# A stack of four layers with a state-space scan: C's rows through DRAM, softplus as one ScalarE function, and one program without a loop

## The chip, the cores and the metric

The kernel runs on one core of one Trainium2 chip. The metric is the device time of one execution in microseconds. "Profiled execution" means one execution that the hardware profiler recorded; its "span" runs from the first to the last instruction.

## The reference

The input is 32 images of 128 channels and 56 x 56 pixels, in float32. Each image passes four layers. Before each layer the image is normalized over groups of channels.

1. A dynamic convolution: the channel means choose a mixture of four 128 x 128 matrices, and the result goes through one depthwise 3 x 3 kernel at dilations 1, 3 and 5, with a silu after each.
2. A spline of every pixel's value.
3. A linear attention over an 8 x 8 grid, with a depthwise convolution.
4. A Mamba layer over the 3136 pixels in order. The change lies here. Cut to what matters:

```python
xc = silu(conv1d(xin) + conv_b)                   # 256 inner channels
dbl = xc @ x_proj_w.T                             # 8 columns dt, 16 of B, 16 of C
delta = softplus(dbl[:, :8] @ dt_proj_w.T + dt_proj_b)
dA  = exp(delta[..., None] * A)                   # 256 channels x 16 states
dBu = delta[..., None] * B[:, :, None, :] * xc[..., None]
h_t = dA_t * h_{t-1} + dBu_t                      # along the pixels
y_t = einsum('bdn,bn->bd', h_t, C_t)
out = ((y + xc * D) * silu(z)) @ out_proj_w.T
```

## The kernel before

**Chunks and steps.** An image is cut into 7 chunks (`NCH`) of 448 pixels (`CH`), 224 chunks in all. The scan of a chunk takes 16 steps (`STEPS`): 256 channels in two halves (`db`, 0 or 1), and 16 states in 8 pairs (`p`). In one step the 128 partitions hold 64 channels twice, once for each state of the pair, and two such blocks stand side by side, so that a tile is 128 x 2 x 448. A step does this:

- `b_rows`: TensorE spreads the two rows of B over the 128 partitions, from `dbl` (the high and the low parts of dt, B and C, as float32r) by a selection matrix `sel`, into the one PSUM buffer `pb`.
- `decay`: ScalarE makes the two `da` tiles, exp(delta times A), in three PSUM buffers.
- `state`: VectorE multiplies `du` (delta times x) by `pb` into `h`, and scans `h` twice along the pixels.
- `products`: ScalarE saves the last column, and GpSimd multiplies `h` by the rows of C (`cb`) into `hc`.
- `add`: TensorE sums `hc` over the states into `y`. After the last pair of a half VectorE multiplies by the gate, `sz`.

In the steps of the first half `c_rows` also makes the `cb` tile of a pair: TensorE spreads the rows of C by `sel` as it does B's, and ScalarE copies the result from PSUM into one of nine buffers (`NPAIR + 1`). The second half uses the same eight tiles.

**The inputs of the next chunk.** `ssm_inputs` (line 989) prepares the next chunk during the steps of this one: the convolution and silu give `xc`, a matmul gives `dbl`, and softplus gives `delta`. Softplus is made as max(v, 0) on VectorE plus ln(1 + exp(-|v|)): Abs, Exp and Ln on ScalarE, and a sum on GpSimd, which also multiplies by `xc`. All of this stands on 128 different channels in the partitions. So 16 transfers within SBUF of 64 rows (112 KB each) then bring `delta` and `du` into the doubled form. `layer_norm` for the chunk after is put between, so that its Ln shares one switch of ScalarE's function table with that of softplus.

**Order.** Nothing is issued as it is written. `Plan` records every instruction with a price (`price`, line 163) and a step at which it is wanted, and then writes out one order for each engine: it takes, for each engine, what can start first by its prices. Each engine carries out its queue in that order. While the scan of one image goes on, the plan fills in the spline and attention of the next image (`rest`) and the first layer of the image after that (`layer0`). `PREP` says how the pieces of `ssm_inputs` are spread over the steps. All instructions that were recorded so have one line number in the profile, 325.

**DMA.** All transfers are issued by SP. Convolutions read their rows from DRAM (`padded`) into `stack`, as four transfers each, the last being a single row of ones (`onesd`); the spline reads 16 transfers of 32 rows from `xt`.

**Images.** The first image and the first layer of the second come ahead. Then a loop on the device (line 1263) runs five times over six images each (`UNROLL`), and the last two images follow it:

```python
    with tc.For_i(0, B - 2, unroll) as i:
        images(i, unroll, True)
    images(B - 2, 2, False)
```

The functions that the change touches, and those that call them:

Of the kernel before, what the change touches and what calls it, by code (L numbers as in the profile page):

```python
# [26 lines left out]
PW = W + 2 * HALO  # L27
UNROLL = 6

PREP = 17.5  # L30
REST = 92
# [63 lines left out]
class Plan:  # L95
# [67 lines left out]
    def price(self, w, engine, method, args, kw):  # L163

        n = args[0].free_size()
        if method == "dma_start":
            w.cost += 0.35
            w.bytes += 4 * n * args[0].partition_size()
        elif engine == "tensor":
            n = args[2].free_size() if method == "matmul" else n  # L170
            w.cost += max(0.06, n * (5e-4 if args[2].dtype == F32R else 1.8e-3))
        elif engine == "scalar":
            if method == "activation" and args[2] in (AF.Exp, AF.Tanh, AF.Ln):
                w.table = "ln" if args[2] == AF.Ln else "exp"
            columns = sum(isinstance(kw.get(k), bass.AP) for k in ("bias", "scale"))
            w.cost += 0.06 + 8.34e-4 * n + 0.09 * columns + 0.03 * (args[1].space != bass.MemoryType.PSUM)
        elif engine == "gpsimd":
            if n <= 8:
                w.cost += 0.52 if ALU.pow in args else 0.15
            else:  # L180
                slow = method != "tensor_scalar" or ALU.add not in args
                w.cost += 0.14 + n * (1.2e-3 if not slow else 2.12e-3 if method != "tensor_scalar" else 3.8e-3)
        elif method == "tensor_tensor_scan":
            w.cost += 0.11 + 2.085e-3 * n
        else:
            if method == "tensor_reduce" or method == "bn_stats":
                n = args[1].free_size()
            w.cost += 0.08 + 1.02e-3 * n
# [161 lines left out]
def tile_conv_stack(ctx: ExitStack, tc: tile.TileContext, out: bass.AP, x: bass.AP, w: dict):  # L350
# [44 lines left out]
    xprojT = load("xprojT", [P, DI, P])  # L395
    dtb = load("dtb", [P, DI])
    amat = load("alog", [P, NB, NPAIR])
# [15 lines left out]

    ones4 = const.tile([P, NST], F32, name="ones4")
    nc.vector.tensor_add(ones4[:], ident[:, 0:NST], ident[:, LOW : LOW + NST])
    for r in (C_ROW, C_ROW + LOW):
        nc.vector.tensor_add(ones4[:], ones4[:], ident[:, r : r + NST])
    sel = const.tile([P, NST, Q], F32R, name="sel")
    nc.vector.tensor_copy(sel[:], ones4[:].unsqueeze(2).to_broadcast([P, NST, Q]))

    low = load("low", [P, 2])
    dtT = const.tile([P, DI * P], F32R, name="dtTr")
    dtw = setup(DI * P, name="t")
    nc.sync.dma_start(dtw[:], w["dtT"])
    nc.vector.tensor_copy(dtT[:], dtw[:])
    nc.vector.scalar_tensor_tensor(dtT[:], dtT[:], low[:, 1:2], dtw[:], ALU.mult, ALU.add)

# [96 lines left out]

    cbT = const.tile([P, DI * P], F32R, name="cbT")
    cbw = setup(DI * P, name="g")
    nc.vector.memset(cbw[:], 0.0)
    for r in (0, 32):
        nc.sync.dma_start(cbw[r : r + 1, :], w["convb"])
    nc.vector.tensor_scalar_mul(cbw[:], cbw[:], 0.5)  # L530
    nc.vector.tensor_copy(cbT[:], cbw[:])
    nc.vector.tensor_sub(cbT[32:33, :], cbw[32:33, :], cbT[32:33, :])
    onesr = const.tile([P, 1], F32R, name="onesr")
# [7 lines left out]
    xns = [const.tile([P, CH + DCONV - 1], F32, name=f"xn{k}") for k in range(3)]  # L541
    dbls = [const.tile([P, CH], F32R, name=f"dbl{k}") for k in range(2)]
    xcs = [const.tile([P, DI, CH], F32, name=f"xc{k}") for k in range(2)]
    halves = [[const.tile([P, 2, CH], F32, name=f"{n}{k}") for k in range(3)] for n in ("delta", "du")]

    sz = const.tile([P, DI, CH], F32, name="sz")
    delta = const.tile([P, DI, CH], F32, name="delta")
    du = const.tile([P, DI, CH], F32, name="du")

    padded = [dramp.tile([P, PW * PW], F32, name=f"padded{k}") for k in range(2)]
    onesd = dramp.tile([1, NG * ROWS * PW], F32, name="onesd")
    zero = setup(HALO * PW, name="t")
    nc.vector.memset(zero[:], 0.0)
# [9 lines left out]

    plan.pitch = {pd[:].tensor.name: PW * PW for pd in padded} | {onesd[:].tensor.name: NG * ROWS * PW}
    nc = plan

# [375 lines left out]
    def norm_weights(st, ctr, cb):  # L944
# [5 lines left out]
        nc.vector.tensor_scalar_mul(cb[:], pm, -1.0)  # L950
    def layer_norm(xt, xn, j, norm, before=None, other=None):


        if norm is None:
            nc.scalar.activation(other, other, AF.Ln, bias=one[:, 0:1])
            return
        ctr, cb = norm
# [8 lines left out]
        rstd = tmp.tile([P, CH], F32, tag="v", name="rstd")  # L966
        with plan.together():
            nc.scalar.activation(rstd[:], pv, AF.Ln, bias=lneps[:, 0:1])
            if other is not None:
                nc.scalar.activation(other, other, AF.Ln, bias=one[:, 0:1])  # L970
            nc.scalar.activation(rstd[:], rstd[:], AF.Exp, scale=-0.5)
        nc.gpsimd.tensor_mul(rstd[:], cen[:], rstd[:])
# [16 lines left out]
    def ssm_inputs(xt, k, norm):  # L989
# [3 lines left out]
        for db in range(DI):  # L993
            ch = slice(db * P, (db + 1) * P)
            ps = psum()
            for i in range(DCONV):
                nc.tensor.matmul(ps, winT[:, i, ch], xn[:, i : i + CH], start=(i == 0), stop=False)
            nc.tensor.matmul(ps, cbT[:, ch], onesr[:].to_broadcast([P, CH]), start=False, stop=True)
            silu(xc[:, db, :], ps)
            yield 3.3  # L1000
        ps = psum()
        for db in range(DI):
            nc.tensor.matmul(ps, xprojT[:, db, :], xc[:, db, :], start=(db == 0), stop=(db == DI - 1))
        nc.scalar.copy(dbl[:], ps)
        nc.vector.scalar_tensor_tensor(dbl[:], dbl[:], low[:, 0:1], ps, ALU.mult, ALU.add)
        yield 1.7

        for db in range(DI):
            ps = psum()
            nc.tensor.matmul(ps, dtT[:, db * P : (db + 1) * P], dbl[:], start=True, stop=True)  # L1010
            nc.scalar.activation(du[:, db, :], ps, AF.Abs, bias=dtb[:, db : db + 1])
            nc.vector.tensor_scalar(delta[:, db, :], ps, dtb[:, db : db + 1], 0.0, ALU.add, ALU.max)
            yield 0.8
        nc.scalar.activation(du[:], du[:], AF.Exp, scale=-1.0)
        layer_norm(xt, xns[(k + 1) % 3], j + 1, norm if j + 1 < NCH else None, xn, du[:])
        nc.gpsimd.tensor_add(delta[:], delta[:], du[:])
        nc.gpsimd.tensor_mul(du[:], delta[:], xc[:])
        yield 4.0

        for db in range(DI):  # L1020
            for src, dst in zip((delta, du), halves):
                dst = dst[(DI * k + db) % 3]
                for s in range(2):
                    for r in range(2):
                        nc.sync.dma_start(dst[Q * s : Q * s + Q, r, :], src[Q * r : Q * r + Q, db, :])
        yield 1.0

    class Scan:
# [11 lines left out]

        def both(self, ps, row, p):

            rows = slice(row, row + 2 * LOW)
            pair = sel[rows, 2 * p : 2 * p + 2, :].rearrange("p a b -> p (a b)")
            nc.tensor.matmul(ps, pair, self.dbl[rows, :], start=True, stop=True)

        def c_rows(self, n):

            db, p = divmod(n, NPAIR)
            if db == 0:  # L1050
                ps = psum()
                self.both(ps, C_ROW, p)
                self.cbs[p] = cbp.tile([P, CH], F32, tag="cb", name="cb")
                nc.scalar.copy(self.cbs[p][:], ps)

        def b_rows(self, n):

            p = n % NPAIR
            self.pbs[n] = ps_bc.tile([P, 512], F32, tag="bc", name="pb")[:, :CH]
            self.both(self.pbs[n], B_ROW, p)  # L1060

# [113 lines left out]
    ov = out.rearrange("b c l -> c b l")  # L1175
    unroll = next(u for u in (UNROLL, 2) if (B - 2) % u == 0)

# [84 lines left out]
    plan.issue()  # L1262
    with tc.For_i(0, B - 2, unroll) as i:
        images(i, unroll, True)
    images(B - 2, 2, False)


def _layout(a):
# [21 lines left out]
    def xproj_columns(v):  # L1290
        m = np.zeros((DI * P, P), np.float32)
        for h in (0, LOW):
            for r in DT_ROWS:
                m[:, h + r : h + r + DTR] = v[:, :DTR]
            m[:, h + B_ROW : h + B_ROW + NST] = v[:, DTR : DTR + NST]
            m[:, h + C_ROW : h + C_ROW + NST] = v[:, DTR + NST :]
        return m

    def dt_rows(v):
        m = np.zeros((P, DI * P), np.float32)  # L1300
        for h in (0, LOW):
            for r in DT_ROWS:
                m[h + r : h + r + DTR] = v
        return m

    def low_rows():
        m = np.zeros((P, 2), np.float32)
        for h in (0, 2 * LOW):
            m[h + LOW : h + 2 * LOW, 0] = -1.0
        for h in (0, LOW):  # L1310
# [28 lines left out]
        "low": low_rows(),  # L1339
        "dtb": halves(a["L3_conv_dt_proj_b"]),  # L1340
        "alog": pairs(a["L3_conv_A_log"]),
# [26 lines left out]
```

## Time and profile before

| | |
|---|---|
| Time, median of 3 runs | 17185.76 us (17185.5 to 17192.23) |
| Profiled execution, time | 17194.07 us |
| Its span | 17192.1 us |
| TensorE matmul busy | 14998.2 us, 87% |
| VectorE busy | 14452.2 us, 84% |
| ScalarE busy | 11730.3 us, 68% |
| GpSimd busy | 10788.9 us, 63% |
| DMA, mean over 16 engines | 39.0% of the span, 92 GB/s |
| Mean granted TensorE clock | 0.885 |

In the profile PE is TensorE, PEld its weight loads, DVE VectorE, ACT ScalarE, POOL GpSimd, and SPq the queue of SP, which issues the transfers. An instruction is named by what it writes and reads, `out<-in`. A group's row gives its shape and number, then the busy time in us and the mean ns of one, then the idle time of its engine just before, with what ended that idle time. The row of a window gives, for each engine, busy time and instructions, and at the end the granted clock, the mean share of the 16 DMA engines and GB/s. The part of the span before the loop takes about 495 us, each turn of the loop about 3150 us, and the last two images the rest.

### The profile page before, as it was taken

Reading aid. Unit: us, or ns where it says so; the run is one execution under the profiler, and the core shown is the slowest. Engines: PE = TensorE matmul, PEld = TensorE weight load, DVE = VectorE, ACT = ScalarE, POOL = GpSimd, SP = SyncE. Lnnn points to the kernel's source line nnn. Section 1 sums busy time; section 2 is a strip of 40 time slices with the busy share of each in tenths; the row PEclk is TensorE's granted clock in tenths of the full one; section 3 lists DMA queues with packets and bytes.
Section 4 is the critical chain, followed back from the end, with each engine's and each line's share of the span. In section 5 each row is a group of like instructions: output and inputs, shape, how many; then the busy total and the mean of one; then the engine's idle time right before and its main releaser. Section 6 shows DMA issues by size and latency. Waiting matters only on the chain. (4 is left out here: it accounts for less than half of the span.)

```text
span 17192.1 us, 216067 instructions
## 1 busy us (share of the span) xinstructions
PE 14998.2 (87%) x68192; PEld 4866.0 (28%) x68192; DVE 14452.2 (84%) x17314; ACT 11730.3 (68%) x21127; POOL 10788.9 (63%) x6406
## 2 busy tenths in 40 slices
PE   6888998888988888988889888889888898888888
PEld 1222222222222222222222222222222222222222
DVE  2788888888888888888888888888888888888889
ACT  3666677766677666777666776667776667766675
POOL 1566666666666666666666666666666666666666
PEclk7888898989998888989899888899888999888887
DMA  4443443434433444434344334444343443344421
GB/s 105 105 96 94 101 98 84 98 89 97 106 89 87 96 96 97 100 84 98 91 96 106 93 82 96 95 102 98 85 97 88 98 106 91 85 98 95 94 55 31
DMA packets 986167, 1590.09 MB, mean 92 GB/s; under 512 B 175621, under 2 KB 611208, under 8 KB 984330
## 3 DMA queue, kind: packets, MB, share of 16 engines
q1 hardware_dynamic: 985002, 1576.06, 39.0%
q8 instruction: 548, 8.98, 0.2%
q14 instruction: 617, 5.05, 0.1%
HBM read 785.62 MB, written 173.18 MB: 56 GB/s over the span
## 5 line engine op out<-in xcount | busy, mean ns | idle before, releaser
L325 POOL TENSOR_TENSOR hc<-h,cb 128x896 f32<-128x896 f32 x3584 | 7480.6, 2092 | 5035.7 <-DVE h L325 2490.3
L325 DVE TENSOR_TENSOR_SCAN h<-da,last,h 128x448 f32<-128x448 f32 x6144 | 6811.5, 1138 | 628.5 <-ACT da L325 530.6
L325 ACT ACTIVATE da<-delta,alog 128x448 f32<-128x448 f32 x7168 | 4490.6, 633 | 2043.6 <-DVE h L325 1843.0
L325 DVE TENSOR_TENSOR h<-du,pb 128x896 f32<-128x896 f32 x3584 | 3838.3, 1071 | 422.3 <-PE pb L325 179.9
L325 PE MATMUL y<-hc,sums 128*64 128x448 f32 x14336 | 3937.6, 628 | 283.7 <-POOL hc L325 279.3
L325 PE MATMUL pb<-dbl,sel 64*128 64x448 f32 x3584 | 1841.4, 514 | 626.6 <-DVE h L325 584.6
L325 PE MATMUL mm<-xn,winT 128*128 128x448 f32 x3584 | 1782.4, 605 | 172.0 <-DVE sz L325 129.5
L325 PE MATMUL mm<-stack,dsT 96*32 96x448 f32 (+1 forms) x16128 | 1877.0, 576 | 58.2 <-DMA stack<-onesd 23.5
L325 ACT ACTIVATE hats<-stack,bia,scl 128x448 f32<-128x448 f32 x2688 | 1894.2, 755 | 13.0 <-DVE bia L325 10.0
L325 PE MATMUL mm<-hats,wspl 128*32 128x448 f32 x12544 | 1476.4, 574 | 130.7 <-DVE xt L325 68.5
L325 PEld LDWEIGHTS pb<-dbl,sel 64*128 64x128 f32 x3584 | 714.6, 199 | 2985.3 <-DVE h L325 1877.5
L325 PEld LDWEIGHTS y<-hc,sums 128*64 128x64 f32 x14336 | 800.6, 146 | 2063.1 <-issue 971.8
L325 ACT ACTIVATE t<-mm 128x448 f32<-128x448 f32 x1568 | 816.5, 536 | 791.0 <-PE mm L325 780.4
L325 ACT COPY cb<-mm 128x448 f32<-128x448 f32 x1792 | 927.9, 529 | 568.0 <-PE mm L325 456.2
L325 PE MATMUL mm<-dbl,sel 64*128 64x448 f32 x1792 | 874.1, 517 | 476.1 <-ACT cb L325 139.4
L325 ACT ACTIVATE hats<-hats,one 128x1344 f32<-128x1344 f32 x896 | 1261.2, 1408 | 1.2
L325 ACT COPY last<-h 128x2 f32<-128x2 f32 x3072 | 579.0, 188 | 815.6 <-DVE h L325 790.3
L325 DVE TENSOR_TENSOR_SCAN h<-da,h 128x448 f32<-128x448 f32 x1024 | 1064.3, 1074 | 54.5 <-ACT da L325 46.5
L325 POOL TENSOR_TENSOR xt<-xt,g 128x448 f32<-128x448 f32 x672 | 765.1, 1139 | 341.9 <-DVE g L325 330.4
L325 PEld LDWEIGHTS mm<-xn,winT 128*128 128x128 f32 x3584 | 613.1, 199 | 1026.5 <-issue 662.5
L325 DVE SCALAR_TENSOR_TENSOR g<-t,mm 128x448 f32<-128x448 f32 x672 | 410.5, 611 | 406.1 <-ACT t L325 403.4
L325 PEld LDWEIGHTS mm<-stack,dsT 96*32 96x32 f32 (+1 forms) x16128 | 429.6, 113 | 1127.7 <-issue 875.2
(187 smaller groups left out, 15891.8 us busy)
## 6 DMA issues: line engine op xcount, KB each, us to landing
stack<-padded SPq DMA_DIRECT2D x2688, 264.0 KB
stack<-xt SPq DMA_DIRECT2D x3584, 56.0 KB
delta<-delta SPq DMA_DIRECT2D x1792, 112.0 KB
du<-du SPq DMA_DIRECT2D x1792, 112.0 KB
padded<-yc SPq DMA_DIRECT2D x224, 264.0 KB
padded<-yc SPq DMA_DIRECT2D x256, 231.0 KB
xt<-x_dram SPq DMA_DIRECT2D x224, 224.0 KB
out_dram<-xt SPq DMA_DIRECT2D x224, 224.0 KB
```

Of the source, the lines that this page charges most:

```text
L325: call()
```

## The change

**C's rows.** `dbl` keeps dt and B alone, in 64 partitions. The 16 rows of C are copied by ScalarE into `ct` and written to DRAM (`crow`, two buffers); each `cb` tile is then read from there by one transfer, which repeats each of two rows for 64 partitions.

**Softplus.** The weights of dt are doubled beforehand, so that a matmul gives the doubled form at once: four matmuls per chunk where there were two, and a ScalarE function Softplus straight into the `delta` that the scan reads. Only `xc` is doubled by DMA (`xds`, eight transfers of 64 rows per chunk), and GpSimd makes `du` from both. `layer_norm` moves ahead of this and no longer shares a group with softplus.

**Images.** `images(0, B, False)` records all 32 images as one plan; there is no loop on the device.

**Prices.** The plan's price of a float32r matmul is raised, softplus has a table of its own in it, and `PREP` is 16.0.

```diff
-UNROLL = 6
-PREP = 17.5
+PREP = 16.0
...
-            w.cost += max(0.06, n * (5e-4 if args[2].dtype == F32R else 1.8e-3))
+            w.cost += 0.16 + 5e-4 * n if args[2].dtype == F32R else max(0.06, 1.8e-3 * n)
...
+    crows = [dramp.tile([NST, CH], F32, name=f"crow{k}") for k in range(2)]
...
-        with plan.together():
-            nc.scalar.activation(rstd[:], pv, AF.Ln, bias=lneps[:, 0:1])
-            if other is not None:
-                nc.scalar.activation(other, other, AF.Ln, bias=one[:, 0:1])
-            nc.scalar.activation(rstd[:], rstd[:], AF.Exp, scale=-0.5)
+        nc.scalar.activation(rstd[:], pv, AF.Ln, bias=lneps[:, 0:1])
+        nc.scalar.activation(rstd[:], rstd[:], AF.Exp, scale=-0.5)
...
             silu(xc[:, db, :], ps)
+            with plan.together():
+                for h in range(2):
+                    for r in range(2):
+                        nc.sync.dma_start(xds[db][Q * h : Q * h + Q, r, :], xc[Q * r : Q * r + Q, db, :])
...
-        nc.scalar.copy(dbl[:], ps)
-        nc.vector.scalar_tensor_tensor(dbl[:], dbl[:], low[:, 0:1], ps, ALU.mult, ALU.add)
+        ct = tmp.tile([P, CH], F32, tag="v", name="ct")
+        nc.scalar.copy(ct[C_ROW : C_ROW + NST, :], ps[C_ROW : C_ROW + NST, :])
+        nc.sync.dma_start(crows[k % 2][:], ct[C_ROW : C_ROW + NST, :])
+        nc.scalar.copy(dbl[:], ps[: 2 * LOW, :])
+        nc.vector.scalar_tensor_tensor(dbl[:], dbl[:], low[: 2 * LOW, 0:1], ps[: 2 * LOW, :], ALU.mult, ALU.add)
         yield 1.7
+        if j + 1 < NCH:
+            layer_norm(xt, xns[(k + 1) % 3], j + 1, norm, xn)
+        yield 3.0
         for db in range(DI):
-            ps = psum()
-            nc.tensor.matmul(ps, dtT[:, db * P : (db + 1) * P], dbl[:], start=True, stop=True)
-            nc.scalar.activation(du[:, db, :], ps, AF.Abs, bias=dtb[:, db : db + 1])
-            nc.vector.tensor_scalar(delta[:, db, :], ps, dtb[:, db : db + 1], 0.0, ALU.add, ALU.max)
-            yield 0.8
-        nc.scalar.activation(du[:], du[:], AF.Exp, scale=-1.0)
-        layer_norm(xt, xns[(k + 1) % 3], j + 1, norm if j + 1 < NCH else None, xn, du[:])
-        nc.gpsimd.tensor_add(delta[:], delta[:], du[:])
-        nc.gpsimd.tensor_mul(du[:], delta[:], xc[:])
-        yield 4.0
-
-        for db in range(DI):
-            for src, dst in zip((delta, du), halves):
-                dst = dst[(DI * k + db) % 3]
-                for s in range(2):
-                    for r in range(2):
-                        nc.sync.dma_start(dst[Q * s : Q * s + Q, r, :], src[Q * r : Q * r + Q, db, :])
-        yield 1.0
+            delta, du = (h[(DI * k + db) % 3] for h in halves)
+            for r in range(2):
+                b = 2 * db + r
+                ps = psum()
+                nc.tensor.matmul(ps, dtT[:, b * P : (b + 1) * P], dbl[:], start=True, stop=True)
+                nc.scalar.activation(delta[:, r, :], ps, AF.Softplus, bias=dtb[:, b : b + 1])
+            nc.gpsimd.tensor_mul(du[:], delta[:], xds[db][:])
+            yield 1.5
...
             if db == 0:
-                ps = psum()
-                self.both(ps, C_ROW, p)
                 self.cbs[p] = cbp.tile([P, CH], F32, tag="cb", name="cb")
-                nc.scalar.copy(self.cbs[p][:], ps)
+                rows = crows[self.k % 2][2 * p : 2 * p + 2, :]
+                nc.sync.dma_start(self.cbs[p][:], rows.unsqueeze(1).to_broadcast([2, Q, CH]))
...
-    with tc.For_i(0, B - 2, unroll) as i:
-        images(i, unroll, True)
-    images(B - 2, 2, False)
+    images(0, B, False)
```

## The prediction

> **What bounds the kernel now.** I read the page first: the busy times and the DMA queues.
>
> ```profile
> PE 14998.2 (87%) x68192; PEld 4866.0 (28%) x68192; DVE 14452.2 (84%) x17314; ACT 11730.3 (68%) x21127; POOL 10788.9 (63%) x6406
> ...
> q1 hardware_dynamic: 985002, 1576.06, 39.0%
> ```
>
> Two engines are nearly full: TensorE at 87%, VectorE at 84%. Over 224 chunks the span is 76.75 us per chunk, VectorE works 64.5 us of it, and each of the 16 DMA engines is busy 0.39 x 76.75 = 29.9 us. Next the timeline, for the distance from one `h<-du,pb` to the next: averaged over all chunks, steps 0 to 6 of a chunk take 3.6 to 4.7 us, steps 7 to 13 take 4.7 to 5.1, steps 14 and 15 take 5.7 and 6.7. A step needs 1071 + 2 x 1138 ns = 3.35 us of VectorE before any other work, so the early steps have no slack on VectorE; most of its 12 us of idle time per chunk lies in the late ones. So what leaves VectorE pays, what leaves another engine pays only through a wait of VectorE. The chain of waits covers only the last quarter of the span (it adds up to 23%) and mixes TensorE, VectorE and ScalarE, so I do not build on it.
>
> The groups by form (busy us, mean ns, then idle before them):
>
> ```profile
> L325 DVE TENSOR_TENSOR_SCAN h<-da,last,h 128x448 f32<-128x448 f32 x6144 | 6811.5, 1138 | 628.5 <-ACT da L325 530.6 <-ACT cb L325 0.5 <-ACT last L325 0.5
> L325 ACT COPY cb<-mm 128x448 f32<-128x448 f32 x1792 | 927.9, 529 | 568.0 <-PE mm L325 456.2 <-PE pb L325 105.1 <-POOL hc L325 2.7
> L325 PE MATMUL mm<-dbl,sel 64*128 64x448 f32 x1792 | 874.1, 517 | 476.1 <-ACT cb L325 139.4 <-DVE g L325 92.8 <-ACT cen L325 78.3
> L325 ACT ACT_TABLE_LOAD x512 | 656.9, 1283 | 8.8
> L325 DVE TENSOR_SCALAR delta<-mm,dtb 128x448 f32<-128x448 f32 x448 | 298.5, 677 | 166.7 <-ACT du L325 150.3 <-PE mm L325 11.5
> L325 ACT ACTIVATE du<-mm,dtb 128x448 f32<-128x448 f32 x448 | 276.7, 632 | 322.2 <-PE mm L325 287.0 <-DMA stack<-xt 20.5 <-DVE delta L325 11.1
> L325 PE MATMUL mm<-dbl,dtTr 128*128 128x448 f32 x448 | 210.7, 495 | 20.9 <-ACT cen L325 13.9 <-DVE dbl L325 1.3
> ```
>
> The fifth row disappears with the change, with the 166.7 us that VectorE stood idle before it; rows two, three and six price what ScalarE and TensorE lose and gain. Then VectorE's waits and those of SP's queue (total, times, longest):
>
> ```profile
> DVE h L325 <- ACT da L325: 577.0, 443, 4.4
> ...
> DVE h L325 <- DMA du<-du: 104.2, 43, 4.7
> ```
>
> ```profile
> SPq L325 <- DMA stack<-padded: 287.5, 337, 4.3
> ```
>
> ScalarE's `da` is the largest wait of VectorE; SP already waits for landings of its own earlier transfers.
>
> **The change, part by part.** The sum is made against the profiled execution, 17194.07 us, which is 8 us over the median. About 0.2% is what a measurement of this kernel can tell from no change.
>
> VectorE: 448 `delta` instructions go, 298.5 us, all on the path. Of the 166.7 us idle before them I take half, since the wait for ScalarE may reappear at the next instruction: -298 - 83 = -381 us (ends -298 and -465).
>
> ScalarE: the copies of `cb` (927.9 us), Abs (276.7), Exp (213.0) and Ln (231.6) go, 1649 us. Added: 896 softplus at the 632 ns of `du<-mm,dtb`, the same shape with a bias column, 566 us; 224 copies of 16 rows at the 530 ns of `dbl<-mm`, 119 us; and table loads. The built program has 1437 of them where 515 run now: Ln and softplus no longer share a switch, and softplus comes in two pairs, each between two loads. 922 x 1283 ns = 1183 us. Net +219 us, off the path by itself, as ScalarE is busy 68%. What counts is that during a switch no `da` is made: 2 x 1283 + 2 x 632 = 3.8 us, with three `da` buffers for cover. One such stretch a chunk, 4.2 us long (load, 634, 1034, load), now goes with 577 us of waits, 2.58 us per chunk. Two more of them cost between 0 and 2 x 2.58 us. ScalarE gets 4.1 us of copies lighter per chunk, so I take 0.65 each: 224 x 1.3 = +291 us (0 to +1156). [...]
>
> TensorE: 1792 broadcasts of C go (874 us), 448 more `dtT` matmuls at 495 ns come (+222). VectorE waits for TensorE some 840 us in all (`xt` 368, `pb` 180, `sz` 126, `rden` 89, `kb` 74); 652 of TensorE's 14998 us gone may take an eighth of them: -100 (0 to -450, above half of these waits). The reordering by the planner's new price and by PREP lies within these ends.
>
> GpSimd: two products of 128x896 per chunk before and after, about 2088 ns each. But `du<-delta,xd` now waits on GpSimd's queue for softplus and for the copies of `xc`; behind it stand the `hc` products, for which TensorE's `y` waits. The `du` transfer that VectorE waits for (104 us) goes. Taken as -50 (-104 to +104).
>
> The loop: VectorE in the 40 us before and over a boundary:
>
> ```profile
> 3600.00:3640.00 40.00, 38.46 (x181) 11.76 (x174) 36.55 (x41) 23.48 (x39) 24.93 (x16) 1.00 0.12 27
> 3640.00:3680.00 40.00, 24.52 (x51) 7.45 (x51) 26.02 (x28) 17.51 (x32) 22.75 (x14) 0.59 0.34 78
> ```
>
> 36.55 - 26.02 = 10.5 us lost, at five boundaries: -53 us (0 to -67, the gap without `h` being 13.4 us).
>
> Without DMA: 17194 - 381 + 291 - 100 - 50 - 53 = 16,900 us.
>
> DMA. All transfers stay on SP's queue, about as many. Per chunk 16 transfers of 64 rows go and 8 come (`xd`), a row of 1792 B each time; plus `crow`, 16 rows, and 8 of `cb`, 128 rows each. What a row costs one DMA engine (last two columns: share of the 16 engines, GB/s):
>
> ```profile
> 14.00:15.00 1.00, 0.00 (x0) 0.00 (x0) 0.97 (x8) 0.00 (x0) 0.00 (x0) 1.00 0.91 274
> 15.60:18.60 3.00, 0.00 (x0) 0.00 (x0) 2.76 (x21) 1.21 (x2) 0.00 (x0) 1.00 0.97 316
> 3650.50:3654.50 4.00, 3.42 (x8) 0.59 (x8) 3.85 (x5) 0.00 (x0) 4.00 (x4) 0.56 0.80 176
> 9175.86:9176.20 0.34, 0.34 (x1) 0.12 (x2) 0.34 (x1) 0.00 (x0) 0.34 (x1) 1.00 0.06 25
> ```
>
> The first row is mostly the load of `winT`, one DRAM row read for 128 partitions: broadcasting from DRAM is no slower in itself. Loads of x run at 316 GB/s with all engines busy, 16 x 1792 / 316 = 91 ns per row; the third row is `delta` and `du`, copies within SBUF: 16 x 0.80 x 1792 / 176 = 130 ns. The last is one `stack<-onesd`, a transfer of a single row: 0.06 of the engines, which is one of 16, at 25 GB/s, or 72 ns for 1792 B. So a transfer is divided by its outer rows, and one with one row is not spread.
>
> Every wide transfer of the trace has at least 32 rows outermost on both sides. `cb<-crow` has 128 on the SBUF side, but its source stands as 2 rows, each repeated 64 times. I take it as nearest to the one-row case: two engines, 64 rows each, 64 x 72 to 130 ns = 4.6 to 8.3 us per transfer. [...] No row of this trace has an outermost count of 2.
>
> Spread over 16 engines, `cb` would add 8 x 8 rows = 4.6 to 8.3 us per chunk to 29.9 - 8.3 + 4.2 = 25.8: about 32 us of 75, hidden as now. On two engines it adds 512 rows, 37 to 67 us: these two are busy 63 to 92 us of 75. I take 80 ns, between the one-row case and a full load, as the two run mostly alone: 41 + 26 + 1 (the `onesd` rows) = 68 us. That fits on average, but not where it falls. In the built order the eight `cb` follow `crow` with, on average, 6.5 `stack<-xt`, 4.4 `stack<-padded`, 1.4 `onesd` and 0.8 `padded` between them, some 8 us on each engine: 49 us of work. They can't start before `hc` frees the buffers of the last chunk (nine buffers, eight in use), one per step from step 8: 41.5 us at today's steps, less when `crow` is late. Work for the two engines so runs 8 us behind, or up to 27 if `crow` comes at step 12 (22 us left). Behind it on SP stand the stack loads, and each transfer also waits for the one eight before it. What they have in hand:
>
> ```profile
> 9168.49 0.29 SPq L325 DMA_DIRECT2D stack<-onesd  x1
> 9187.42 2.48 PE L325 MATMUL mm<-stack,dsT 97*32 97x448 f32 x24
> ```
>
> This load was issued 19 us before its first matmul; over the 672 of layer 0 the median is 20.0 us, a quarter under 10.0, and landing takes up to 6 of it. With a delay of 8 to 27 us the tighter quarter is late by several us, and TensorE's queue is in order: the matmul that waits holds up `pb`, and VectorE with it. I take 5.5 us per chunk (0 to 27, the whole backlog): 224 x 5.5 = +1232 us.
>
> Sum: 16,900 + 1232 = 18,132, rounded 18,130 us.
>
> **The rivals.** *Hidden after all* (not slower): `cb` is spread, or the loads' lead swallows the delay. For it: the median lead of 20 us, and only 43 us of TensorE's waits for `stack` transfers now; against it: the one-row transfer. It decides if `cb` lands in about 1 us, or if the delays stay under the lead of the loads behind. 16,900 us, from 16,100 with all gains at their good ends.
>
> *ScalarE*: transfers hidden, but both new stretches cost the full 2.58 us. For it: the `da` wait is VectorE's longest now; against: ScalarE gets lighter just there. 16,900 - 291 + 1156 = 17,765 us.
>
> *The two engines become the bound*: rows at 130 ns. 92 + 1 = 93 us per chunk, 224 x 93 + 495 (the part before the loop) = 21,300 us. For it: rows are that slow under load now; against: then all 16 engines are busy, here two.
>
> **How the numbers follow.** Forecast 0.68 (0.03 of it faster, 0.02 same), its own range 17,300 to 19,300; hidden 0.20 (0.17 faster, 0.01 same, 0.02 slower); ScalarE 0.07; the two engines 0.05. Faster 0.2, same 0.03, slower 0.77. From 16,800 to 19,300 some 0.07 of the hidden case lies below, and the last rival with 0.08 of the forecast above.
>
> **What would show it.** Right: waits of SP, TensorE (`stack`) or GpSimd (`hc`) for `cb` and `stack` transfers of over 1000 us together; the mean DMA share about 0.4 in spite of 13% more bytes; softplus near 632 ns, table loads at 1283 ns; no `delta` row on VectorE. Wrong: no such waits and a chunk under 75 us (spread), or `da` waits of over 1500 us (ScalarE).

## The result, and the profile after

| | before | after |
|---|---|---|
| Time, median | 17185.63 us (17180.34 to 17192.23, 4 runs) | 18729.22 us (18725.25 to 18739.89, 4 runs) |
| Span of the profiled execution | 17192.1 us | 18738.1 us |
| Per chunk (span / 224) | 76.75 us | 83.65 us |
| Mean granted TensorE clock | 0.885 | 0.837 |

The ratio is 1.0899, with a 95% interval of 1.088 to 1.0918. The kernel is slower by 1,544 us; the forecast was 18,130 us, slower, with a range of 16,800 to 19,300.

The busy times and the main DMA queue, from the page of the changed kernel:

```profile
PE 15094.9 (81%) x66848; PEld 4783.1 (26%) x66848; DVE 14226.0 (76%) x16864; ACT 12056.9 (64%) x20481; POOL 10785.8 (58%) x6406
...
q1 hardware_dynamic: 1081706, 1787.91, 37.2%
```

VectorE has 226 us less to do, ScalarE 327 us more, and yet every engine's share has fallen: all of them wait more. The DMA engines carry 13% more bytes (1787.91 MB against 1576.06) in a span that is 9% longer, and their mean share has gone down from 39.0% to 37.2%. A mean over 16 engines cannot show that a few of them are full.

The groups of the changed kernel by form (busy us, mean ns, then idle before them):

```profile
L324 ACT ACT_TABLE_LOAD x1434 | 1839.8, 1283 | 29.8 <-PE mm L324 2.9
L324 ACT ACTIVATE delta<-mm,dtb 128x448 f32<-128x448 f32 x896 | 532.3, 630 | 15.0 <-PE mm L324 7.3
L324 PE MATMUL mm<-stack,dsT 97*32 97x448 f32 x5376 | 723.6, 612 | 876.3 <-DMA stack<-onesd 680.2 <-DMA stack<-padded 184.1 <-DVE g L324 7.0
L324 DVE TENSOR_TENSOR h<-du,pb 128x896 f32<-128x896 f32 x3584 | 3838.4, 1071 | 1460.1 <-PE pb L324 1387.5 <-POOL du L324 25.8 <-ACT da L324 24.1
```

Softplus takes 630 ns, and the table loads take 1283 ns each with 29.8 us of idle time before 1,434 of them. The `delta` row of VectorE is gone. The third row tells the story: the matmul that reads the last of the four `stack` transfers now has 876 us of idle time before it, where it had 58.2:

```profile
L325 PE MATMUL mm<-stack,dsT 97*32 97x448 f32 x5376 | 681.9, 580 | 58.2 <-DMA stack<-onesd 23.5 <-ACT cb L325 16.9 <-DMA stack<-padded 13.7
```

The fourth is what follows: `h` waits for `pb`, whose matmul stands behind the stack matmuls in TensorE's queue. Laid over each other in the trace, TensorE itself waited for `stack` transfers during 512 of these 1,387.5 us and worked on stack matmuls during 297; in the kernel before that was 0 and 17 of 180 us.

VectorE's waits (total, times, longest):

```profile
DVE h L324 <- PE pb L324: 1387.5, 535, 16.6
DVE h L324 <- ACT da L324: 636.0, 352, 5.5
...
DVE st L324 <- DMA xt<-x_dram: 556.3, 29, 20.9
```

In the kernel before the wait for `pb` was this:

```profile
DVE h L325 <- PE pb L325: 179.9, 173, 3.6
```

The wait for `da` was 577.0 and is hardly longer, so ScalarE's switches are not where the time went. The `st` row is new: the statistics of a new image wait for the load of x, some 19 us for each of 29 images. SP's queue issues those loads too, and its own waits show why they are late:

```profile
SPq L324 <- DMA cb<-crow: 1057.9, 482, 6.2
SPq L324 <- DMA stack<-padded: 559.7, 600, 5.3
```

SP has waited for `stack<-padded` before (287.5 us), and never for C. What one group of `cb` looks like is seen in SP's timeline of the changed kernel (start, duration):

```profile
6907.32 2.38 SPq L324 DMA_DIRECT2D xd<-xc  x4
6911.51 0.34 SPq L324 DMA_DIRECT2D crow<-ct  x1
6913.06 18.39 SPq L324 DMA_DIRECT2D cb<-crow  x6
6939.95 5.43 SPq L324 DMA_DIRECT2D stack<-xt  x8
```

Issuing six `cb` transfers takes 18.39 us: the first three issues take 0.55, 0.54 and 0.48 us, the last three 2.28, 2.87 and 4.17, and these end 1.4, 1.3 and 1.2 us after the landing (6920.94, 6925.60 and 6930.28 us) of the `cb` transfer that was issued three before. That they wait for it is inferred from these times. The window over that stretch (engines' busy times, granted clock, share of the 16 DMA engines, GB/s):

```profile
6915.00:6938.00 23.00, 16.26 (x66) 5.33 (x65) 21.32 (x29) 19.52 (x31) 17.44 (x10) 0.53 0.13 48
```

The share is 0.13, which is 2 of 16, at 48 GB/s: 24 GB/s for an engine, so 75 ns for a row of 1792 B and 64 x 75 ns = 4.8 us for one transfer of 224 KB. Counted over the whole trace, exactly two packets are in flight during 38.4% of the span, against 0.9% in the kernel before. Per chunk, that is where it hurts: steps 1 to 4, just behind the `cb` group, take 8.61, 7.37, 5.22 and 4.85 us, against 4.73, 3.86, 3.98 and 3.58 before.

### The profile page after: what moved, and what is told of

Same layout as the page of the kernel before. It is cut to its first block, busy times and chain, and to the rows that moved or that the text cites. A ratio compares the mean times of both kernels' runs of the same rounds, so it can differ in the third digit from the quotient of the medians.

```text
span 18738.1 us, 212473 instructions
## 1 busy us (share of the span) xinstructions
PE 15094.9 (81%) x66848; PEld 4783.1 (26%) x66848; DVE 14226.0 (76%) x16864; ACT 12056.9 (64%) x20481; POOL 10785.8 (58%) x6406
## 3 DMA queue, kind: packets, MB, share of 16 engines
q1 hardware_dynamic: 1081706, 1787.91, 37.2%
## 4 chain that ended last, share of the span: by engine, by line
PE 39%; DMA 19%; DVE 15%; ACT 13%; issue 5%; SPq 5%; POOL 4%; POOLq 0%; DVEq 0%; ACTq 0%
PE mm L324 27%; DVE h L324 11%; PE y L324 8%; DMA cb<-crow 8%; ACT hats L324 6%; SPq L324 5%; DMA stack<-onesd 4%; PE pb L324 3%; POOL hc L324 3%; DMA stack<-padded 3%; ACT da L324 2%; DMA padded<-yc 2%; ACT L324 2%; DMA xt<-x_dram 1%; DVE ws L324 1%
## 5 line engine op out<-in xcount | busy, mean ns | idle before, releaser
L324 DVE TENSOR_TENSOR h<-du,pb 128x896 f32<-128x896 f32 x3584 | 3838.4, 1071 | 1460.1 <-PE pb L324 1387.5
L324 PE MATMUL y<-hc,sums 128*64 128x448 f32 x14336 | 4061.2, 654 | 646.1 <-POOL hc L324 644.4
L324 PE MATMUL mm<-stack,dsT 96*32 96x448 f32 (+1 forms) x16128 | 2025.8, 619 | 876.3 <-DMA stack<-onesd 680.2
L324 PE MATMUL mm<-xn,winT 128*128 128x448 f32 x3584 | 1966.1, 655 | 63.4 <-DVE xc L324 38.0
L324 ACT ACT_TABLE_LOAD x1434 | 1839.8, 1283 | 29.8 <-PE mm L324 2.9
L324 POOL TENSOR_TENSOR du<-delta,xd 128x896 f32<-128x896 f32 x448 | 932.3, 2081 | 218.0 <-ACT delta L324 189.0
L324 DVE BATCH_NORM_STATS2 st<-xt 128x6 f32<-128x448 f32 x896 | 545.8, 617 | 618.7 <-DMA xt<-x_dram 556.3
L324 PEld LDWEIGHTS mm<-xn,winT 128*128 128x128 f32 x3584 | 664.0, 216 | 1035.8 <-issue 775.5
```

The source lines that it names most:

```text
L324: call()
```

## The experiments

The theory: a `cb` transfer runs on as many DMA engines as its source has outermost rows, two, and the transfers queued behind it come late. The rivals: ScalarE's table switches; the new order that the planner writes; the missing loop.

### The number of engines: 4 and 16 rows in place of 2

The rows of C are written to DRAM several times, so that the source of `cb` has more outermost rows. The bytes that `cb` brings are the same.

```diff
+    COPIES = 8                                   # 2 with four rows
-    crows = [dramp.tile([NST, CH], ...
+    crows = [dramp.tile([NST * COPIES, CH], ...
...
-        nc.sync.dma_start(crows[k % 2][:], ct[C_ROW : C_ROW + NST, :])
+        nc.sync.dma_start(crows[k % 2][:].rearrange("(s c) f -> s c f", c=COPIES),
+            ct[C_ROW : C_ROW + NST, :].unsqueeze(1).to_broadcast([NST, COPIES, CH]))
...
-                rows = crows[self.k % 2][2 * p : 2 * p + 2, :]
+                rows = crows[self.k % 2][2 * COPIES * p : 2 * COPIES * (p + 1), :]
-                nc.sync.dma_start(self.cbs[p][:], rows.unsqueeze(1).to_broadcast([2, Q, CH]))
+                nc.sync.dma_start(self.cbs[p][:], rows.unsqueeze(1).to_broadcast([2 * COPIES, Q // COPIES, CH]))
```

Four rows ("the run before" is the one with sixteen rows, which comes next):

> As the run before, with each row of C twice in DRAM, so that the source stands as 4 rows repeated 32 times. Theory A: 32 rows of 75 ns on each of four engines, 2.4 us per transfer, windows with cb alone at a DMA share of 4/16 = 0.25; the burst of eight is 19 + 8 = 27 us against some 40 us of steps, so most of the loss goes: 16,900 to 17,300 us. Theories B and C: above 18,300 us.

Measured: 17,179.1 us in one run. Exactly four packets are in flight during 18.9% of the span, where the changed kernel has two during 38.4%: twice the engines, half the time.

Sixteen rows:

> The changed kernel, but crow holds each row of C eight times in DRAM (one transfer of 16 rows of SBUF, each written eight times), so that the source of a cb transfer stands as 16 rows repeated 8 times, not 2 rows repeated 64 times. Number of transfers, their waits and the bytes of cb stay; 196 KB more are written per chunk. Theory A (a cb transfer runs on as many engines as its outermost count): cb costs 8 rows on each engine, the backlog goes, about 16,900 us (16,500 to 17,200), windows with cb alone at a DMA share far above 0.13. Theory B (the way through DRAM costs by its order: crow's landing, then cb, on one queue): stays above 18,300 us. Theory C (softplus and the table loads cost the time): stays above 18,300 us.

Measured: 17,008.62 us (16,996.13 to 17,018.16); the ratio to the kernel before is 0.991, 0.9893 to 0.9926. With C's bytes spread, the whole change becomes a small gain, 0.9%.

The runs bear the theory out for two rows (a share of 0.13, which is two engines) and for four (four packets in flight). For sixteen the share of 0.72 in a window of the last kernel below shows that many more engines work than two, but not how many.

The kernel with sixteen rows doesn't have the order of the changed kernel, though. The write to DRAM is larger, the planner prices it by its bytes, and so it writes another order for all engines. What an order is worth came out only in the runs on C below, and so the last run repeated this one with the order held. In it the planner prices the write as in the changed kernel; the queues of TensorE, VectorE, ScalarE and GpSimd are then the changed kernel's, row by row.

```diff
-            w.bytes += 4 * n * args[0].partition_size()
+            w.bytes += 4 * n * args[0].partition_size() // (8 if "crow" in args[0].tensor.name else 1)
```

> The spread version again (C's rows eight times in DRAM), but with the write to DRAM priced by the planner as in the changed kernel, so that the order of the instructions on TensorE, VectorE, ScalarE and GpSimd is that of the changed kernel row by row, and SP's too but for the place of one early stack transfer. In the spread version before (17,009 us) the planner had written another order, and the kernels without C show that an order alone is worth several hundred us. Theory (the engines that a transfer occupies decide): 17,009 us or the 17,261 us of the changed kernel without C, 16,900 to 17,350 us: 1,400 to 1,800 us of the change's loss are the two engines' alone. Rival (the order made a large part of what the spreading seemed to gain): 17,700 to 18,500 us.

Measured: 16,597.53 us (16,588.29 to 16,603.09), ratio 0.9657, 0.964 to 0.9673. That is below the range of the theory. At one and the same order, two rows in place of sixteen cost 18,729 - 16,598 = 2,132 us, more than the whole loss of the change. And the two spread versions, with the same instructions but for two table loads, in two orders, are 411 us apart.

The kernel with four rows turns out to have the changed kernel's order too: in its trace the queue of SP is the same row by row, and 14 of TensorE's 66,848 rows differ, in one short stretch. So at one order the time is 18,729 us with two rows, 17,179 with four (one run) and 16,598 with sixteen, and with it fall VectorE's wait for `pb` (1,387.5, 458.4 and 320.1 us) and that of `st` for x (556.3, 214.7 and none). The waits in the kernel with sixteen rows at that order, VectorE's, then TensorE's:

```profile
DVE h L324 <- ACT da L324: 625.9, 372, 4.9
DVE xt L324 <- PE mm L324: 470.2, 299, 22.3
DVE h L324 <- PE pb L324: 320.1, 376, 2.4
```

```profile
PE mm L324 <- DMA stack<-onesd: 25.4, 20, 2.1
PE mm L324 <- DMA stack<-padded: 18.8, 10, 5.3
```

Against the changed kernel the wait for `pb` is shorter by 1,067 us, TensorE's wait for `onesd` falls from 680.2 to 25.4, and the wait of `st` for x is not in the list any more (-556). These two of VectorE's waits make 1,624 of the 2,152 us between the spans. Steps 1 to 4 of a chunk take 6.65, 4.37, 3.88 and 3.87 us: 7.3 of the 9.5 us per chunk come back right there. A window over four `cb` transfers shows them on far more engines, with a share of 0.72 where it was 0.13:

```profile
6911.50:6914.50 3.00, 3.00 (x14) 1.53 (x13) 3.00 (x4) 2.11 (x5) 1.43 (x2) 1.00 0.72 211
```

### C's rows by matmul, with all the rest of the change

`dbl` and `sel` take in C again as in the kernel before, `ct` and `crow` go, and `c_rows` has its matmul and copy back.

```diff
...
-                rows = crows[self.k % 2][2 * p : 2 * p + 2, :]
-                nc.sync.dma_start(self.cbs[p][:], rows.unsqueeze(1).to_broadcast([2, Q, CH]))
+                ps = psum()
+                self.both(ps, C_ROW, p)
+                nc.scalar.copy(self.cbs[p][:], ps)
```

> The changed kernel with C's rows made as before (TensorE and a ScalarE copy), softplus as one function and no loop kept. Theory A: no cb transfers, so no backlog; from the terms of the prediction 17,194 - 381 + 291 - 50 - 53 = 17,000 us, and some more since TensorE has the two more matmuls without the relief: 16,900 to 17,300 us. Theory B: the same. Theory C: above 18,300 us.

Measured: 17,822.81 us (17,815.83 to 17,841.44), ratio 1.0381, 1.0364 to 1.0398. This missed. Without any of C's transfers the change is still slower than the kernel before, by 3.8%. Its busy times, from the page:

```profile
PE 15802.8 (89%) x68640; PEld 5021.0 (28%) x68640; DVE 14223.6 (80%) x16866; ACT 12646.7 (71%) x21981; POOL 10812.8 (61%) x6406
```

TensorE is busy for 1,200 us more than in the last kernel above. By the groups 934 us of it are the matmuls for C, and the same other matmuls take 590 us longer (groups overlap, so the two add up to more); the mean granted clock is 0.847 against 0.880. The two kernels also differ in their order, so no run shows what taking C's rows from TensorE is worth by itself; and why this kernel is slower than the kernel before stays open.

### C's rows by DMA, in the kernel before

Here the old softplus and the loop stay, and only C goes through DRAM, in two outermost rows as in the change and in sixteen. `ct`, its copy and its write to `crow` come in as in the change; `dbl` keeps its rows of C.

```diff
...
-                ps = psum()
-                self.both(ps, C_ROW, p)
-                nc.scalar.copy(self.cbs[p][:], ps)
+                rows = crows[self.k % 2][2 * p : 2 * p + 2, :]
+                nc.sync.dma_start(self.cbs[p][:], rows.unsqueeze(1).to_broadcast([2, Q, CH]))
```

> The kernel before with only C's rows taken from crow by DMA, 2 rows repeated 64 times; softplus and loop as before. Theory A: two engines are busy 29.9 + 38.6 + 1 = 69.5 us of a chunk, more than in the changed kernel (64), as delta and du are still copied: 18,300 to 19,300 us. Theory B: 18,000 to 18,800 us. Theory C: 17,000 to 17,200 us.

Measured: 20,270.59 us in one run, worse than either expectation. In this kernel 16 transfers of `delta` and `du` stand in the same queue, and VectorE waits for those most (the waits of VectorE):

```profile
DVE h L325 <- DMA du<-du: 1147.9, 131, 34.6
...
DVE h L325 <- DMA cb<-crow: 285.1, 29, 22.6
```

That fits the theory, with another victim: what is queued behind `cb` is late. The same with sixteen rows:

> The kernel before, softplus and loop as they were, with only C's rows from DRAM, read as 16 rows repeated 8 times. From the runs so far: C's way spread over 16 engines gained 17,823 - 17,009 = 814 us on the changed kernel. If that gain belongs to C's rows alone, 17,167 - 814 = 16,350 us (16,200 to 16,700). If it was only a gain because the changed softplus had made TensorE and ScalarE the bound, less than half of it: 16,800 to 17,100 us.

Measured: 17,744.24 us (17,741.03 to 17,769.74), ratio 1.0333, 1.0315 to 1.035: 1,400 us over the first expectation and above the second, although the wait for `du<-du` is back at 90.7 us. TensorE has 1,792 matmuls fewer than before (though its busy time is 115 us longer) and ScalarE 639 us less to do, and the kernel is slower. The suspicion was that it is the transfers, or else the order. So C was left out altogether, first in the kernel before:

```diff
-            if db == 0:
-                ps = psum()
-                self.both(ps, C_ROW, p)
-                self.cbs[p] = cbp.tile([P, CH], F32, tag="cb", name="cb")
-                nc.scalar.copy(self.cbs[p][:], ps)
+            self.cbs[p] = cfix                   # a constant tile of ones
```

> The kernel before without C's rows at all: h is multiplied by a tile of ones in place of the broadcast rows, so neither the matmul (1,792), nor the copy (1,792 x 529 ns = 928 us of ScalarE), nor any transfer for C is done. It stands against the kernel before with C through DRAM, spread over 16 rows (17,744 us). Theory A (the added transfers, and the SP queue in which they stand, cost the 560 us that it is slower than the kernel before): the work itself is worth what it is in the changed kernel, 814 us, so about 16,350 us, at most 16,700. Theory B (with C's work gone, the order that the planner writes for the rest is worse, whatever the transfers do): 17,400 to 17,800 us.

Measured: 17,384.19 us in one run, at the edge of theory B and far from A. With 1,792 matmuls and 1,792 copies gone and nothing put in their place, the kernel before becomes 206 us slower. VectorE's and GpSimd's busy times are what they were (14,446.5 and 10,784.5 us against 14,452.2 and 10,788.9). The instructions that are left stand in another order, and the matmuls among them take 316 us longer by the groups, at a mean clock of 0.865 against 0.885; the run doesn't say whether the order or the clock comes first. The remaining 360 us to the version with spread transfers may be the transfers or again the order; no run separates these.

The changed kernel without C:

> The changed kernel without C's rows at all: h is multiplied by a tile of ones, with no copy, no write to DRAM and no transfer for C. It stands against the spread version of the changed kernel (17,009 us). Theory (transfers on 16 engines are hidden, as the prediction's sum without DMA has it): 16,850 to 17,010 us. Rival (1,792 transfers of 229 KB cost time on 16 engines too, through the stack transfers that they delay or the queue): 16,300 to 16,700 us.

Measured: 17,261.13 us in one run, above both ranges: it is 253 us slower than the spread version with C and 664 us slower than the same with the changed kernel's order. An order, with the clock that comes with it, is thus worth up to several hundred us in this kernel, in either direction. Every comparison in this document that does not hold the order has an error of that size.

### The loop

Only the loop is taken out of the kernel before.

```diff
-    with tc.For_i(0, B - 2, unroll) as i:
-        images(i, unroll, True)
-    images(B - 2, 2, False)
+    images(0, B, False)
```

> The kernel before with all images in one plan and nothing else changed. By the prediction's term -53 us (five boundaries of 10.5 us), so 17,100 to 17,120 us. Rival: the longer plan puts the loads of x later (VectorE's st waits 188 to 206 us for them in the runs without the loop, 0 in the kernel before), and the time is 17,200 to 17,400 us.

Measured: 17,113.35 us (17,098.36 to 17,117.07) against 17,182.29 for the kernel before, ratio 0.9961, 0.9946 to 0.9975: -69 us, inside the first range. The order is nearly held here: 67,030 of TensorE's 68,192 rows stand at the same place in both traces. The `st` wait for x is not there, so one long program alone doesn't make the loads of x late.

### The table switches

Abs takes the place of Softplus, one for one and at the same shape; one takes 630 and 626 ns in the two runs, where Softplus took 630 and 632, and 446 table loads are left. `delta` is then |v| and not softplus(v).

```diff
-                nc.scalar.activation(delta[:, r, :], ps, AF.Softplus, bias=dtb[:, b : b + 1])
+                nc.scalar.activation(delta[:, r, :], ps, AF.Abs, bias=dtb[:, b : b + 1])
```

In the kernel with C by matmul:

> As the run with C by matmul, with Abs in the place of Softplus (delta is then not softplus): same instruction count and duration, but no switch of ScalarE's table, about 515 loads, not 1,430. Theory D (the extra loads make the softplus part slower): the 656 us over the kernel before go, 17,000 to 17,300 us. Theory E (TensorE: 448 more matmuls at an order that the plan makes denser; its busy time rose from 14,998 to 15,803 us): stays at 17,600 to 17,850 us.

Measured: 16,656.03 us in one run, below both ranges and 1,167 us less, for 1,366 - 446 = 920 loads fewer (1,180 us). In the version with sixteen rows:

> As the run with C spread over 16 engines, with Abs in the place of Softplus: the loads of ScalarE's table that softplus needs go. The prediction's term for them is 291 us, with ends 0 and 1156: 16,720 us by the term; 17,000 if they cost nothing; 16,350 or less if theory D holds in full here too.

Measured: 16,128.47 us in one run, 880 us less, as theory D had it, for 1,432 - 446 = 986 loads fewer (1,265 us). Both look as if a switch cost 0.7 to 1 times its full 1283 ns. But the planner knows of the tables too, so that these orders differ as well. A third kernel keeps softplus and drops the switches: it writes ln(1 + exp(v)), with Exp in the place of Softplus, and the Ln of both halves in one group with the layer norm's, which moves behind the four Exp.

```diff
-                nc.scalar.activation(delta[:, r, :], ps, AF.Softplus, bias=dtb[:, b : b + 1])
+                nc.scalar.activation(deltas[db][:, r, :], ps, AF.Exp, bias=dtb[:, b : b + 1])
...
+        with plan.together():
             nc.scalar.activation(rstd[:], pv, AF.Ln, bias=lneps[:, 0:1])
+            for o in others:
+                nc.scalar.activation(o[:], o[:], AF.Ln, bias=one[:, 0:1])
             nc.scalar.activation(rstd[:], rstd[:], AF.Exp, scale=-0.5)
```

> The kernel with C's rows eight times in DRAM (17,009 us), with softplus of the doubled channels written as Ln(1 + Exp(x)): the Exp from PSUM takes the place of Softplus one for one, and the two Ln of a chunk stand beside the layer norm's Ln, so that one switch of the table serves all of them. Table loads fall from about 1,435 to about 515: 920 x 1283 ns = 1,180 us of ScalarE; 448 activations of 128x896 at 1,034 ns come in: 463 us. Theory (the switches cost nearly their full price, 881 us for 989 loads in the kernel with Abs): -820 us for the loads, and +230 us (half of the 463) for the added Ln: 16,420 us, between 16,190 and 16,650; faster than both kernels. Rival (a switch lies in idle time of ScalarE and costs little, and what the kernels with Abs gained came from the order of the work): 16,950 to 17,400 us.

Measured: 16,608.84 us (16,595.94 to 16,622.96), ratio 0.9668, 0.9652 to 0.9684. It is 400 us faster than the spread version it was made from, inside the theory's range, with 920 table loads fewer and 448 activations more; and it is equal to the spread version in the changed kernel's order, which has all 1,434 loads. The 400 us are no more than an order gave there. What a switch costs in the end is not settled.

## Why the prediction was right, and where its sizes were off

**The mechanism** was right, and each mark that it named is there: the waits of SP for `cb` and `stack<-padded` (1,618 us), of TensorE for the stack transfers (872) and of GpSimd for `cb` (324), instead of 1,000 together; the share of 0.37 in spite of 13% more bytes; 630 ns; 1283 ns; no `delta` row (these last three would be there under any rival). The rival with hidden transfers is excluded by the window at 0.13; the ScalarE rival by the `da` wait, 636 us where it needed over 1,500, and by the kernel with sixteen rows at the same order, which keeps all 1,434 table loads and is 2,132 us faster; the two engines as the bound by 75 ns a row where it needed 130.

**The stall behind `cb`** was the term that was mis-sized: 5.5 us per chunk (0 to 27) against 2,132 / 224 = 9.5 measured at the same order. The rate was nearly right (80 ns taken, 75 measured). What was left out of "what is queued behind it" is the load of x: it too stands in SP's queue, and costs VectorE 556 us, 2.5 us per chunk. Of the other 7 us, 4.8 are the longer wait for `pb` (1,067 us), which the prediction did name by way of the stack transfers; the rest is spread over smaller waits of VectorE, such as `xt` for TensorE (139 us) and `xc` for ScalarE (95).

**The sum without DMA** was 16,900 us, 294 under the kernel before; the spread version at the changed kernel's order is 594 under it. So the two misses, of -900 and +300 us, partly cancel, and the forecast is 600 us below the measured time; that it is no further off is luck. The +300 is also within what an order alone gave (411). Of the 606 us between the two spans, 275 are busy time of VectorE (298 forecast) and 331 are idle time. In that idle time the waits for `delta` (150) and for `du<-du` (104) are gone, as the terms for VectorE and GpSimd had it. The `da` wait is only 49 us longer (577.0 to 625.9), where the switch term put +291. In the runs with Abs the same wait is shorter by 184 us (576.4 to 392.7, with C by matmul) and by 244 (595.2 to 351.4, with sixteen rows), which is near the term, but the whole time fell by 1,167 and 880. No two of the kernels compared here have one order, so the size of this term stays open.

**TensorE's relief** was priced at -100 us from an eighth of its waits. The runs can't give its size: C's rows by matmul against spread transfers is 814 us (17,823 - 17,009) in two orders, and C left out altogether, in a third, is slower than C by DMA. That the planner's order "lies within these ends" (0 to -450) was the weak sentence of this part: an order moved the time by 411 us with the same instructions but for two table loads, and the kernel before lost 206 us when work was taken away from it.

**The loop**: -53 forecast, with ends at 0 and -67; -69 measured, with some 25 us of uncertainty either way.

## What to carry to other kernels

Ask of every transfer how many rows stand outermost at its source, for a broadcast from DRAM above all: here two rows, each repeated for 64 partitions, gave a share of 0.13, and sixteen, each repeated for 8, gave 0.72. If they are few, write the source several times, and look for the share that a window shows during it rather than for the mean. Then list everything that is issued behind it in the same queue, not only the transfer that is late most often. Where a planner writes the order, an edit of work or price can also shuffle the rest: hold the order in the comparison, or treat differences of some per cent as unexplained; and the version to keep here is the change with C's rows eight times in DRAM, in the changed kernel's order, 3.4% faster than the kernel before (0.964 to 0.9673).

## What was not expected of the hardware

Behind a stall, TensorE worked at half its clock here. The timeline of TensorE in the changed kernel shows four matmuls of one form before and during the `cb` group above, 0.97 us for the four at first and 1.76 us later, and 1.99 us of idle time between (start, duration):

```profile
6911.82 0.97 PE L324 MATMUL y<-hc,sums 128*64 128x448 f32 x4
6914.78 0.47 PE L324 MATMUL pb<-dbl,sel 64*128 64x448 f32 x1 [1.99 <-DVE h L324]
...
6920.10 1.76 PE L324 MATMUL y<-hc,sums 128*64 128x448 f32 x4
```

In the windows around them the granted clock is 1.00 and 0.50 (the first column after the length is TensorE's busy time):

```profile
6911.00:6915.00 4.00, 2.01 (x7) 0.55 (x7) 4.00 (x6) 2.95 (x7) 3.42 (x4) 1.00 0.05 8
6919.00:6923.00 4.00, 4.00 (x9) 1.49 (x9) 4.00 (x8) 3.21 (x6) 4.00 (x3) 0.50 0.12 45
```

TensorE is busy for half of the first window, its clock falls after that, and the second window, full of matmuls, runs at a clock of 0.50. Over the whole span the changed kernel's 66,848 matmuls take 15,094.9 us and the same ones in the same order, with C spread, 14,602.7: 492 us more busy time, at a mean clock of 0.837 against 0.880. The granted clock takes only the values 0.5 and 1 in the traces of the kernel before and of the changed kernel; it is 0.5 during 33% of the changed kernel's span and, worked out from the mean of 0.880 with these two values, 24% of the other. How much of the 492 us lies on the path wasn't measured, and neither was why one order gets a better clock than another. In the first of the two windows TensorE is busy for 2.01 of 4.00 us and idle for at most 1.99 us at a time, and the clock fell after it; whether the idle time was the cause isn't shown.
